# Gated layer: transposed latent scores placed later between the gated pieces than the other latent steps

## The chip, the cores and the metric

The kernel runs on one core of one Trainium2 chip, in one launch. The metric is the device time of one execution in microseconds; each kernel is executed several times and the median counts. A further execution is recorded by the hardware profiler, and all views and rows below come from that one.

## The reference, cut to what matters

The program is a model of four layers on x (4 sequences of 512 tokens with 256 features). Each layer normalises x and adds an attention part and a feed-forward part. Only the third layer (index 2) is touched by the change:

```python
xn = _layernorm(x, axis=-1)
x = x + _L2_attn_ref(xn, ...) + _L2_ffn_ref(xn, ...)
```

`_L2_attn_ref` is a gated recurrent attention with 16 heads. Keys, values, queries, slot scores `s` and gates are products of `xn`; the slot weights are `exp(s)` over a running sum, and the recurrences over time give a softmax over 64 slots and then the values:

```python
p = jnp.exp(s - z)                      # z: cumulative log-sum-exp over time
hk = hk * g_t[:, :, None, :] + k_t[..., None] * p_t[:, :, None, :]
pvT = jax.nn.softmax(okT, axis=-1)
hv = hv * g_t[..., None] + p_t[..., None] * v_t[:, :, None, :]
o = o * rsqrt(mean(o * o) + EPS) * g_norm_weight * (g * sigmoid(g))
return o.reshape(b, t, VALUE_DIM) @ Wo
```

`_L2_ffn_ref` begins with a causal attention over latent keys and queries, again with 16 heads of 16 features, and goes on to a shared expert and seven routed ones:

```python
scores = jnp.einsum('bqhd,bkhd->bhqk', q, k) * scale
scores = jnp.where(causal[None, None], scores, jnp.finfo(scores.dtype).min)
probs = jax.nn.softmax(scores, axis=-1)
out = jnp.einsum('bhqk,bkhd->bqhd', probs, v).reshape(b, s, H)
h = x + out @ o_w
out = h + moe(rmsnorm(h, ln2_w), ...)
```

## The kernel before, in words

All products are in float32 on TensorE (PE); one matmul of the program shows as two instructions in the trace. VectorE (DVE), ScalarE (ACT) and GpSimd (POOL) do the element-wise work. Each engine works through its own queue in order. The order in a queue is made when the program is built: instructions are traced in the order of the Python code, and a scheduler places each on its engine when, by its own costs, its inputs are there.

`layer2` computes the gated attention in 32 units. A unit is one pair of heads and one sequence of 512 tokens. While a unit is computed by `gated_unit`, the next unit's projections are made by `gated_supply` and the previous unit's output product by `gated_drain`. All three are generators that yield after a piece of work. `run` takes their pieces in a fixed pattern (`"mmmmsmsmmdmmsmsdmsd"`, 19 pieces of a unit, where m is the unit, s the supply and d the drain) and places steps of a further generator between them, by a credit that starts at zero in each unit:

```python
credit += rate
while credit >= 1:
    credit -= 1
    next(beside, None)
```

For units 0 to 23 this further generator is `latent_chain`, the latent attention with its shared expert, and the rate is `beside` = 0.44. What is left of the chain after unit 23 is traced at once. For the units after that it is the routed experts, at a rate of their own.

`latent_chain` goes over 16 groups: 4 sequences of 4 groups, each with 4 heads. Three stages overlap. In iteration n, `latent_keys` makes `kT` and `qT` of group n, `latent_maxima` works on group n-1 and `latent_values` on group n-2, the latter two in turns of one step each.

- `latent_maxima` computes the scores with the query in the partitions (`qk`, L2158), in three banks: the last query chunk against 512 keys, the chunks of 384 and 128 keys, the chunk of 256 keys. Four tiles, one for each head, are filled at a time. DVE reads each tile with one or two fused instructions that mask it and keep the row's maximum (`junk`, `mx`, L2165). At the end the negated maxima are transposed (`mxt`, L2175) and added to a spare row of `qT` (L2176), so that later scores come out with the maximum subtracted.
- `latent_values` computes the same scores transposed, with the key in the partitions (`kq`, L2190), in three banks of the same sizes (512; 384 with 128; 256). ACT takes the exponential of each of the four tiles (`pr`, L2195), POOL zeroes what lies above the diagonal (L2198). Then `pv` (L2206) is the product with the values, `pvs` (L2212) its copy, and `pvt` (L2216) the transposition back.

All PSUM tiles of the latent chain come from one pool of four buffers, `pw` (tag `w`). A bank of `qk` takes all four, and so does a bank of `kq`. So `kq` of a bank can start only when DVE has read the tiles of `qk` before it, and the next `qk` only when ACT has read those of `kq`. The gated units have a pool of four PSUM buffers of their own.

The gated work that lies between these steps: `pj` (L1763, projections), `turn` (L1794), `sc` (L1826, scores; DVE masks them at L1832), `pt` (L1841, values and gates by tokens), `st` (L1814, sums), `pok` (L1859, L1865), `okt` (L1874), `pvt` (L1894), `pov` (L1905, L1911), `ot` (L1947) and `o` (L1954, added to x by DVE at L1959). On DVE the slot sums run through a scan (L1775) and four reciprocals (L1776), and the softmax over slots through L1878, L1880 and L1883. ACT changes its function table between the exponentials and the silu of the gates (L1890).

Of the kernel before, what the change touches and what calls it, by code (L numbers as in the profile page):

```python
# [14 lines left out]
P = 128  # L15
NB = 4
T = 512
# [29 lines left out]


BLOCK = {0: 0, 1: 512, 3: 896, 2: 1024}
BANKS = ((0, (0,)), (512, (1, 3)), (1024, (2,)))  # L50


# [78 lines left out]
class Net:  # L131
# [1009 lines left out]
    def layer1(self):  # L1141
# [115 lines left out]
        self.stats = self.small  # L1257
        self.ordered.close()

    def arms1(self, m, counts):  # L1260

        which = self.r1["which"]
        index = self.nc.values_load(
            which[0:1, m : m + 1], min_val=0, max_val=len(counts) - 1,
            skip_runtime_bounds_check_because="a count of as many numbers at most",
        )
        for i in self.tc.Switch(index, len(counts)):
            yield counts[i]
# [308 lines left out]
    def layer2(self):  # L1577

        nc, a = self.nc, self.a
        UNITS = 8 * NB

        first, beside = 24, 0.44
        moe = self.moe2
        with ExitStack() as ctx:
            tp = lambda n, bufs, **k: ctx.enter_context(self.tc.tile_pool(name=n, bufs=bufs, **k))
            self.ahead = tp("gaw", 2), tp("gaw2", 2)
            self.weights = weights = {0: self.gated_weights(0)}
            self.gp = gp = {"wk": tp("ga", 1), "wk2": tp("ga2", 2), "ps": tp("gaps", 4, space=PSUM)}  # L1590
            gp["gn"] = gn = gp["wk"].tile([P, 1], F32, tag="gn", name="gn")
            self.load(gn, a["l2_gn"])
            units = {}

            def supplied(u):
                pair, b = 2 * (u // 8) + u % 2, u % 8 // 2
                for _ in norms[b]:
                    pass
                if pair not in weights:
                    weights[pair] = self.gated_weights(pair)  # L1600
                units[u] = {"b": b, "w": weights[pair]}
                return self.gated_supply(units[u])

            def supplies(u):
                yield from supplied(u)

            def normed(b):
                if b:
                    with self.tc.issue_after(marks[b - 1]):
                        for _ in collects[b]:  # L1610
                            pass
                    self.layer_norm(b)
                marks.append(self.mark)
                yield
                self.to_features(
                    gp["ps"], self.xn[:, 4 * b : 4 * b + 4, :], self.xnT[:, :, b * T : (b + 1) * T], tag="ps"
                )
                yield

            def run(u, beside, rate):  # L1620


                supply = supplies(u + 1) if u + 1 < UNITS else iter(())
                gathered = collects.get(u // 2 + 1, iter(())) if u < 6 else iter(())
                drain = self.gated_drain(units[u - 1]) if u else iter(())
                credit = 0.0
                chains = {"m": self.gated_unit(units[u]), "s": supply, "d": drain}
                for n, what in enumerate("mmmmsmsmmdmmsmsdmsd" if u + 1 < UNITS else "mmmmdmmdmmdmmm"):
                    next(chains[what], None)
                    if n % 8 != 7:  # L1630
                        with self.tc.issue_after(marks[min(u // 2, NB - 1)]):
                            next(gathered, None)
                    credit += rate
                    while credit >= 1:
                        credit -= 1
                        next(beside, None)

            marks = []
            collects = {b: self.collect1(b, 5) for b in range(1, NB)}
            norms = [normed(b) for b in range(NB)]  # L1640
            for it in (norms[0], supplied(0)):
                for _ in it:
                    pass
            with ExitStack() as lctx:
                lp = self.lp
                lp["wk"] = lctx.enter_context(self.tc.tile_pool(name="la", bufs=1))
                lp["w"] = lctx.enter_context(self.tc.tile_pool(name="laps", bufs=4, space=PSUM))
                latent = self.latent_chain()
                for u in range(first):
                    run(u, latent, beside)  # L1650
                for _ in latent:
                    pass
            wk = tp("ex", 4)
            gp["ex"] = tp("exps", 4, space=PSUM)
            self.router3()
            routed = self.routed2(wk)
            for u in range(first, UNITS - 2):
                run(u, routed, 1.45)
            for _ in routed:
                pass  # L1660
            run(UNITS - 2, self.ended2(wk, gp["ex"]), 0.75)
            run(UNITS - 1, self.ahead3(gp["ex"]), 1.0)
            drain = self.gated_drain(units[UNITS - 1])
            for chain in (self.units3[0], self.units3[0], drain, self.units3[0], drain, drain):
                next(chain, None)
        self.held.close()
# [381 lines left out]
    def latent_chain(self):  # L2048


        self.latent_tables()
        ready, maxed = None, None
        for n in range(4 * NB + 2):
            values, maxima = maxed, ready
            maxed, ready = maxima, None
            b, g = n // 4, n % 4
            if b < NB:
                if g == 0:
                    yield from self.latent_inputs(b)
                ready = b, g, *self.latent_keys(g)  # L2060
                yield
            steps = []
            if maxima:
                steps.append(self.latent_maxima(*maxima[2:]))
            if values:
                if values[1] == 0:
                    self.latent_va()
                    yield
                steps.append(self.latent_values(*values))
            while steps:  # L2070
                for s in list(steps):
                    if next(s, None) is None:
                        steps.remove(s)
                    yield
            if values and values[1] == 3:
                yield from self.latent_output(values[0])
                yield from self.experts2(values[0])
# [67 lines left out]
    def latent_maxima(self, kT, qT):  # L2145


        nc, lp = self.nc, self.lp
        wk, pw = lp["wk"], lp["w"]
        mx = self.small.tile([P, 4, 4], F32, tag="lmx", name="mx")  # L2150
        for cs in ((3,), (2, 0), (1,)):
            tiles = [pw.tile([P, T], F32, tag="w", name="qk") for _ in range(4)]
            offs = [sum((i + 1) * P for i in cs[:m]) for m in range(len(cs))]
            for off, c in zip(offs, cs):
                m = (c + 1) * P
                for j in range(4):
                    r = slice(32 * j, 32 * j + 32)
                    nc.tensor.matmul(  # L2158
                        tiles[j][:, off : off + m], qT[r, c * P : (c + 1) * P], kT[r, :m], start=True, stop=True
                    )  # L2160
            for j in range(4):
                for off, c in zip(offs, cs):
                    m = (c + 1) * P
                    junk = wk.tile([P, T], F32, tag="q1", name="junk")
                    nc.vector.tensor_tensor_reduce(  # L2165
                        out=junk[:, :m], in0=tiles[j][:, off : off + m], in1=self.hide[:, T - m :],
                        op0=ALU.add, op1=ALU.max, scale=1.0, scalar=NEG, accum_out=mx[:, c, j : j + 1],
                    )
            yield True

        mt = lp["mt"]
        nc.vector.tensor_scalar(mt.rearrange("q c (j r) -> q c j r", r=32)[:, :, :, 16], mx, -1.0, None, ALU.mult)
# [5 lines left out]
    def latent_values(self, b, g, kT, qT):  # L2178

        nc, lp = self.nc, self.lp  # L2180
# [3 lines left out]
        for off, js in BANKS:  # L2184
            m = sum(T - i * P for i in js)
            tiles = [pw.tile([P, T], F32, tag="w", name="kq") for _ in range(4)]
            for i in js:
                for j in range(4):
                    r = slice(32 * j, 32 * j + 32)
                    nc.tensor.matmul(  # L2190
                        tiles[j][:, BLOCK[i] - off : BLOCK[i] - off + T - i * P], kT[r, i * P : (i + 1) * P],
                        qT[r, i * P :], start=True, stop=True,
                    )
            for j in range(4):
                nc.scalar.activation(pr[:, j, off : off + m], tiles[j][:, :m], AF.Exp, scale=0.25)  # L2195
            for i in js:
# [2 lines left out]
                    out=d, in_=d, compare_op=ALU.is_ge, fill=0.0, base=0, pattern=[[0, 4], [1, P]],  # L2199
                    channel_multiplier=-1,  # L2200
                )
            yield True
        pv = pw.tile([P, T], F32, tag="w", name="pv")
        for i in range(4):
            for j in range(4):
# [4 lines left out]
                )  # L2210
        pvs = wk.tile([P, T], F32, tag="pvs", name="pvs")
        nc.scalar.copy(pvs, pv)  # L2212
        yield True
        pt = pw.tile([P, 4, P], F32, tag="w", name="pvt")
        for c in range(4):
            nc.tensor.transpose(pt[:, c, :], pvs[:, c * P : (c + 1) * P], self.ident)  # L2216
# [407 lines left out]
```

## Time and profile before

| | |
|---|---|
| median of 3 runs | 2164.0 us (2156.78 to 2164.17) |
| the profiled execution's own time | 2162.52 us |
| its span, first to last instruction | 2160.8 us |
| mean granted PE clock | 0.931 |
| busy: PE, DVE, ACT, POOL | 1963.7, 1181.5, 831.8, 612.3 us |
| first and last `kq` matmul (L2190) | 505.9 and 1439.5 us from the span's start |

The page divides the span into 40 slices of 54 us and gives the busy share of each engine in tenths. Its groups of instructions name the line, the engine, the operation, what is written and read, the count, the busy time, the mean of one in ns, and after the last bar the idle time of the engine just before them with what ended it. PEld is the loading of weights into PE, which overlaps with the matmuls. The starts and ends of matmuls are modelled: a matmul that waits after it was issued is drawn long. In a view of one line, "sat idle before it until" lists the releasers, each with microseconds and number of times. In the timeline a row is start, length, engine, line, operation, tiles, count, and in brackets the idle time before it.

### The profile page before, as it was taken

Reading aid. Unit: us, or ns where it says so; the run is one execution under the profiler, and the core shown is the slowest. Engines: PE = TensorE matmul, PEld = TensorE weight load, DVE = VectorE, ACT = ScalarE, POOL = GpSimd, SP = SyncE. Lnnn points to the kernel's source line nnn. Section 1 sums busy time; section 2 is a strip of 40 time slices with the busy share of each in tenths; the row PEclk is TensorE's granted clock in tenths of the full one; section 3 lists DMA queues with packets and bytes.
Section 4 is the critical chain, followed back from the end, with each engine's and each line's share of the span. In section 5 each row is a group of like instructions: output and inputs, shape, how many; then the busy total and the mean of one; then the engine's idle time right before and its main releaser. Section 6 shows DMA issues by size and latency. Waiting matters only on the chain.

```text
span 2160.8 us, 35450 instructions
## 1 busy us (share of the span) xinstructions
PE 1963.7 (91%) x13049; PEld 1450.8 (67%) x13049; DVE 1181.5 (55%) x3462; ACT 831.8 (38%) x1688; POOL 612.3 (28%) x727
## 2 busy tenths in 40 slices
PE   6867996689999999999999999989999978899995
PEld 2556875455666766667666676657877866688894
DVE  4886753586655554655565655636556564413223
ACT  2443353323444433434344433342445434425221
POOL 5325652472111111112112111121444451112231
PEclk9958997779999999999999999987999989899998
DMA  9425965320000000000000000102433220267696
GB/s 295 135 98 171 292 186 180 109 67 13 1 1 18 18 11 1 1 1 13 18 11 6 1 1 17 34 11 81 130 117 119 78 73 1 99 210 259 229 335 229
DMA packets 149644, 198.22 MB, mean 92 GB/s; under 512 B 16981, under 2 KB 127672, under 8 KB 149304
## 3 DMA queue, kind: packets, MB, share of 16 engines
q1 hardware_dynamic: 135320, 156.42, 22.3%
q0 software_dynamic: 14112, 39.15, 5.9%
q8 instruction: 111, 1.82, 0.3%
q14 instruction: 101, 0.83, 0.1%
HBM read 154.23 MB, written 41.29 MB: 90 GB/s over the span
## 4 chain that ended last, share of the span: by engine, by line
PE 56%; DVE 9%; issue 7%; POOL 6%; DMA 3%; ACT 2%; another core or an unknown queue 1%; SPq 0%; POOLq 0%; DVEq 0%; ACTq 0%
PE pt L1841 8%; PE pj L1763 6%; PE g L2375 4%; PE o L1954 4%; PE kq L2190 3%; PE sc L1826 3%; PE pov L1905 2%; DVE junk L2165 2%; PE qk L2158 2%; PE o L2388 2%; PE pv L2206 2%; DMA r<-l_rows,in_slot 1%; PE st L1814 1%; PE turn L1794 1%; PE pok L1859 1%
## 5 line engine op out<-in xcount | busy, mean ns | idle before, releaser
L2165 DVE CUSTOM_DVE_ANT_0 junk<-qk,hide 128x512 f32<-128x512 f32 (+3 forms) x256 | 124.5, 486 | 42.2 <-PE qk L2158 25.1
L2198 POOL TENSOR_SCALAR_AFFINE_SELECT pr<-pr 128x512 f32<-128x512 f32 x64 | 40.2, 640 | 339.6 <-ACT pr L2195 339.6
L2375 PEld LDWEIGHTS g<-rT,we 128*128 128x128 f32 x1120 | 132.0, 194 | 5.5 <-ACT rT L382 3.4
L2375 PE MATMUL g<-rT,we 128*128 128x128 f32 x1120 | 132.7, 277 | 2.2 <-ACT rT L382 2.2
L1841 PE MATMUL pt<-Wg,xnT 128*128 128x256 f32 x512 | 124.4, 395 | 2.4 <-DVE both L367 1.0
L349 POOL DMA_INDIRECT r<-l_rows,in_slot x73 | 71.1, 974 | 190.4 <-PE rt L380 106.7
L389 POOL DMA_INDIRECT l_outs<-y,to x73 | 72.1, 988 | 184.9 <-ACT y L388 151.1
L1954 PE MATMUL o<-Wo,oT 128*128 128x256 f32 x512 | 121.9, 381 | 0.0
L1832 DVE TENSOR_TENSOR s<-sc,keep 128x512 f32<-128x512 f32 x128 | 82.5, 683 | 71.8 <-PE sc L1826 68.8
L1841 PE MATMUL pt<-Wv,xnT 128*128 128x256 f32 x512 | 120.7, 387 | 0.0
L1776 DVE RECIPROCAL rz<-rz 128x128 f32<-128x128 f32 x128 | 116.8, 933 | 0.4
L1841 PEld LDWEIGHTS pt<-Wg,xnT 128*128 128x128 f32 x512 | 97.0, 196 | 27.0 <-issue 7.7
L361 DVE TENSOR_TENSOR mine<-r,number 128x2 f32<-128x2 f32 x73 | 13.2, 181 | 179.5 <-DMA r<-l_rows,in_slot 179.4
L2195 ACT ACTIVATE pr<-kq 128x512 f32<-128x512 f32 (+1 forms) x192 | 86.3, 529 | 51.6 <-PE kq L2190 51.2
L1841 PEld LDWEIGHTS pt<-Wv,xnT 128*128 128x128 f32 x512 | 95.3, 191 | 15.2 <-issue 0.2
L1409 POOL DMA_INDIRECT r<-l_rows,in_slot x84 | 82.6, 984 | 67.4 <-PE rt L1421 38.4
L1954 PEld LDWEIGHTS o<-Wo,oT 128*128 128x128 f32 x512 | 96.1, 197 | 8.3 <-issue 0.5
L2190 PE MATMUL kq<-q,kT 32*128 32x128 f32 (+3 forms) x512 | 91.0, 505 | 7.6 <-DVE mx L2165 6.2
L1844 ACT COPY v<-pt 128x512 f32<-128x512 f32 x64 | 37.3, 586 | 127.5 <-PE pt L1841 126.4
L1922 DVE TENSOR_TENSOR o<-pov,g 128x512 f32<-128x512 f32 x64 | 41.3, 686 | 77.0 <-ACT sq L1921 76.0
L2190 PEld LDWEIGHTS kq<-q,kT 32*128 32x128 f32 x512 | 41.7, 197 | 51.4 <-DVE mx L2165 33.8
L1927 POOL TENSOR_TENSOR rs<-ms,sm 128x8 f32<-128x8 f32 x32 | 6.5, 204 | 240.6 <-DVE ms L1925 240.5
(566 smaller groups left out, 4606.3 us busy)
## 6 DMA issues: line engine op xcount, KB each, us to landing
we<-l_w SPq DMA_DIRECT2D x70, 512.0 KB
we<-l_wo SPq DMA_DIRECT2D x35, 512.0 KB
l_outs<-none SPq DMA_DIRECT2D x1, 11776.0 KB
l_outs<-y SPq DMA_DIRECT2D x42, 256.0 KB
we<-l_r_gate SPq DMA_DIRECT2D x38, 128.0 KB
we<-l_r_up SPq DMA_DIRECT2D x38, 128.0 KB
we<-l_r_down SPq DMA_DIRECT2D x38, 128.0 KB
l_rows<-xn SPq DMA_DIRECT2D x8, 544.0 KB
```

The costliest lines, as they stand in the source:

```text
L349: self.nc.gpsimd.indirect_dma_start(out=r[:, m, :], out_offset=None, in_=moe["rows"][:, :], in_offset=bass.IndirectOffsetOnAxis(ap=moe["in ...
L389: self.no_order(moe["name"] + " back", nc.gpsimd.indirect_dma_start(out=moe["outs"][:, :], out_offset=bass.IndirectOffsetOnAxis(ap=to, axi ...
L1409: nc.gpsimd.indirect_dma_start(out=r[:, i, :], out_offset=None, in_=moe["rows"][:, :], in_offset=bass.IndirectOffsetOnAxis(ap=moe["in_slot ...
L1763: nc.tensor.matmul(ps, w[n][:, k, :], self.xnT[:, k, t["b"] * T : (t["b"] + 1) * T], start=(k == 0), stop=(k == KD - 1))
L1776: inverse = lambda c: nc.vector.reciprocal(rz[:, c * P : (c + 1) * P], rz[:, c * P : (c + 1) * P])
L1832: nc.vector.tensor_tensor(s, ps[hh], keep4, ALU.mult)
L1841: nc.tensor.matmul(ps[:, i, :], self.xnT[:, k, s : s + P], w[n][:, k, :], start=(k == 0), stop=(k == KD - 1))
L1954: nc.tensor.matmul(ps[:, p, :], of_parity(oT[:, h, c * D : (c + 1) * D], p), wo[:, h, :], start=(h == 0), stop=(h == 1),)
L2165: nc.vector.tensor_tensor_reduce(out=junk[:, :m], in0=tiles[j][:, off : off + m], in1=self.hide[:, T - m :], op0=ALU.add, op1=ALU.max, sca ...
L2190: nc.tensor.matmul(tiles[j][:, BLOCK[i] - off : BLOCK[i] - off + T - i * P], kT[r, i * P : (i + 1) * P], qT[r, i * P :], start=True, stop= ...
L2195: nc.scalar.activation(pr[:, j, off : off + m], tiles[j][:, :m], AF.Exp, scale=0.25)
L2375: nc.tensor.matmul(pt[:, m, :], we[:, q, k * T + m * P : k * T + (m + 1) * P], rT[:, k, :], start=(k == 0), stop=(k == KD - 1),)
```

## The change

`latent_chain` and its stages now yield a number with each step. `run` takes it off the credit beside the 1 of the step itself: a positive number puts the next latent step later, a negative one puts it earlier. Each bank of `latent_maxima` yields +0.3 (`SPARE`), so that what follows it, the bank of `kq` in `latent_values`, comes later. The bank of `kq` yields -0.1, and the key step, the end of the maxima, the product `pv` and the end of the values yield -0.15 each. Over one full iteration the numbers add up to zero. Steps without a number count as before. The rate goes from 0.44 to 0.455.

Besides, each `kq` matmul is now traced within `issue_after(behind)`, where `behind` is the last PE instruction that was traced before the bank (found by the new method `latest`). This is an edge of order within PE's queue: the scheduler can no longer place the `kq` matmuls ahead of that instruction. No arithmetic is changed.

```diff
+SPARE = 0.3
...
+    def latest(self, engine):
+        engine = getattr(mybir.EngineType, engine)
+        return next(i for i in reversed(self.nc.cur_bb.bb.instructions) if i.engine == engine)
...
-        first, beside = 24, 0.44
+        first, beside = 24, 0.455
...
                     while credit >= 1:
-                        credit -= 1
-                        next(beside, None)
+                        credit -= 1 + (next(beside, None) or 0.0)
...
                 ready = b, g, *self.latent_keys(g)
-                yield
+                yield -SPARE / 2
...
                 for s in list(steps):
-                    if next(s, None) is None:
+                    spare = next(s, None)
+                    if spare is None:
                         steps.remove(s)
-                    yield
+                    yield -SPARE / 2 if spare is None else spare
...
(latent_maxima, after each bank)
-            yield True
+            yield SPARE
...
(latent_values)
             tiles = [pw.tile([P, T], F32, tag="w", name="kq") for _ in range(4)]
+            behind = self.latest("PE")
             for i in js:
                 for j in range(4):
                     r = slice(32 * j, 32 * j + 32)
-                    nc.tensor.matmul(
+                    with self.tc.issue_after(behind):
+                        nc.tensor.matmul(
...
-            yield True
+            yield -SPARE / 3
         pv = pw.tile([P, T], F32, tag="w", name="pv")
...
         nc.scalar.copy(pvs, pv)
-        yield True
+        yield -SPARE / 2
```

In the text below a round is one iteration of `latent_chain` in which both a `qk` and a `kq` group are worked on; there are fifteen. The cover of a bank is the time of the gated matmuls that stand on PE between its `qk` and its `kq`, or between its `kq` and the next `qk`.

More of the change, by code (lines that the diff above doesn't have):

```diff
@@ L2189, in latent_values @@
                     r = slice(32 * j, 32 * j + 32)
[L2190 to L2193, printed above, removed]
+                    with self.tc.issue_after(behind):
+                        nc.tensor.matmul(
+                            tiles[j][:, BLOCK[i] - off : BLOCK[i] - off + T - i * P], kT[r, i * P : (i + 1) * P],
+                            qT[r, i * P :], start=True, stop=True,
+                        )
             for j in range(4):
```

## The prediction

> **What bounds the kernel now.** I read the page first, then the busy time by stretches, then who waits in the stage that the change touches, then the timeline of one bank.
>
> ```profile
> PE 1963.7 (91%) x13049; PEld 1450.8 (67%) x13049; DVE 1181.5 (55%) x3462; ACT 831.8 (38%) x1688; POOL 612.3 (28%) x727
> PE   6867996689999999999999999989999978899995
> L2165 DVE CUSTOM_DVE_ANT_0 junk<-qk,hide 128x512 f32<-128x512 f32 (+3 forms) x256 | 124.5, 486 | 42.2 <-PE qk L2158 25.1
> ```
>
> ```profile
> 500.00:1440.00 940.00, 927.55 (x6432) 630.43 (x6430) 540.47 (x1278) 377.30 (x705) 158.25 (x185) 0.98 0.03 9
> 836.60:843.40 6.80, 6.80 (x31) 3.38 (x30) 0.43 (x1) 2.66 (x5) 1.22 (x2) 0.58 0.00 0
> 952.70:962.90 10.20, 10.20 (x36) 7.63 (x40) 4.34 (x17) 5.06 (x8) 1.22 (x2) 0.55 0.00 0
> 1058.50:1061.90 3.40, 3.40 (x26) 3.14 (x25) 0.00 (x0) 0.78 (x2) 1.22 (x2) 0.67 0.00 0
> ```
>
> The columns of the second fence are length, then busy time of PE, PEld, DVE, ACT and POOL, granted clock, DMA. From 500 to 1440 us the gated units carry the latent chain, and PE is the bound: 927.6 of 940 us. That 99% hides waits, because a matmul that waits for a free PSUM buffer is drawn long. What each scores line waited for, first L2190 (kq), then L2158 (qk), over the run:
>
> ```profile
>   DVE mx L2165: 40.0, 63
> ```
>
> ```profile
>   ACT pr L2195: 4.7, 15
> ```
>
> One bank in the timeline, PE, then DVE, then ACT:
>
> ```profile
> 553.70 1.14 PE L2158 MATMUL qk<-kT,q 32*128 32x512 f32 x8
> 554.77 0.66 PE L1794 MATMUL turn<-ident,kT 128*128 128x128 f32 x4
> 555.26 1.90 PE L1954 MATMUL o<-Wo,oT 128*128 128x256 f32 x8
> 557.09 2.31 PE L2190 MATMUL kq<-q,kT 32*128 32x512 f32 x8
> ```
>
> ```profile
> 555.01 0.68 DVE L2165 CUSTOM_DVE_ANT_0 junk<-qk,hide 128x512 f32<-128x512 f32 x1
> ...
> 558.15 0.08 DVE L2165 DVE_READ_ACCUMULATOR2_ANT mx<- 128x1 f32 x1
> ```
>
> ```profile
> 558.29 1.28 ACT L2195 ACT_TABLE_LOAD   x1 [2.19 <-PE kq L2190]
> 559.59 2.06 ACT L2195 ACTIVATE pr<-kq 128x512 f32<-128x512 f32 x4
> ```
>
> The latent pool has four buffers. qk fills all four, DVE empties them (554.8 to 558.2, 3.4 us), and only 2.3 us of gated matmuls stand before kq. So kq takes 2.3 us instead of the 1.1 us that the same matmuls take where nothing is late. The rule of this stage: **stall = DVE time after qk minus the PE work between qk and kq**. Applied to the fifteen rounds with their three banks it gives 15.1 us for the 512 banks, where the timeline shows 15.7. In all, kq is 44.6 us long-winded in this stage: 15.7 (512), 24.2 (384 with 128), 4.7 (256). That is the most that later scores can win directly.
>
> **The change, part by part.** The order edge on kq holds matmuls behind an earlier matmul of the same queue, so it adds no wait of its own. Rate 0.44 to 0.455: a unit has 19 pieces and credit starts at zero in each, so 8.4 or 8.6 steps become 8 either way. In both built programs the chain's remainder stands behind unit 23. No cost. No DMA moves on SP; POOL swaps one row of selects. Two copies of `a2T` go from DVE to ACT, of about 0.4 us each, under PE's work.
>
> The spares move the kq steps about one piece later and the others earlier. The order in which each program issues on PE, with the gated groups at their durations in the timeline (turn 0.5, half of o 1.7, pt 3.5, pj 1.8, sc 1.1, first pov 1.9), gives the cover between qk and kq, in us, rounds 1 to 15 of the 512 bank. Before: 4.0 2.2 2.1 2.9 4.5 3.6 5.0 2.4 4.0 2.2 2.1 2.9 4.5 3.6 2.1. After: 4.4 3.4 2.1 5.8 6.3 3.6 5.0 4.2 5.0 3.4 2.1 5.8 6.3 3.6 2.9. The timeline starts kq about 0.15 later than these sums.
>
> The DVE side: bare time is 3.4 us for the 512 bank (four maxima 0.85 us apart, as in the timeline above), 4.0 for the 384, 2.2 for the 256. DVE's queue mixes gated work into it. That work, counted between first and last maximum of a bank, is 12.6, 15.7 and 7.7 us over all rounds before, and 14.1, 16.4 and 9.3 after. So the need hardly falls, and the gain is the cover alone.
>
> - 512 banks: rounds 2, 4, 8, 10 and 12 lose their stall. Round 1 keeps 3.2 - 2 x 0.93 (two reciprocals of 934 ns, L1776, fall behind the last maximum) + 0.5 (pvt, no longer ahead) = 1.9. Rounds 3 and 11 are issued as before, 2.0 each. Rounds 9 and 15 keep 0.5 and 0.4. Sum 6.8, gain 8.9.
> - 384 banks: what stays is 1.9, 1.2, 0.5, 4.1, 3.9, 1.2, 0.5, 3.1, 1.3 in rounds 1, 3, 5, 6, 8, 11, 13, 14, 15. Rounds 6 and 14 keep theirs because the maxima queue on DVE behind scan, reciprocals and softmax of the gated unit, and kq stays at the same place against that work. Sum 17.7, gain 6.5.
> - 256 banks: round 7 gets worse, since its first kq has 1.5 us of cover instead of 2.1 and 4.1 us of gated DVE work among its maxima instead of 2.2: about 3.0 for 1.3. Rounds 5 and 13 keep 0.3. Sum 3.6, gain 1.1.
>
> Gain on kq: 16.5 us. Against it stands the other half of the same interval: kq to the next qk, where qk waits for ACT's four exponentials (2.1 us, or 3.5 from kq's end with a table load of 1.28). Cover after for qk 384: 2.3 4.5 4.0 1.6 2.4 1.1 6.3 2.4 2.9 4.5 4.0 1.6 2.4 1.1 4.4. With needs of 2.4 or 3.5 as each round shows now, rounds 4, 5, 6, 8, 9, 12, 13, 14 stall by 1.75, 0.95, 1.15, 0.5, 0.45, 1.75, 0.95, 1.15: 8.7 us, 3.8 now, so 4.9 lost. qk 256 loses 0.45 in three rounds, 1.4. In round 8 ACT is ordered exp, table load, silu, table load, exp: two loads more, 2.6 us on ACT, of which the 2.2 us of PE cover leave about 1. Cost 7.3.
>
> Of the other queues that a kq step is moved past, POOL's selects (0.64 us each) are what pv (L2206) needs: between the last kq and pv stand 3.4 us in rounds 4 and 12, 6.2 before, and the exponentials and the select take about 2.2. Hidden; without that cover it would be 2 us a round. The key steps move earlier, with their products on DVE and the sum on POOL (1.27 us); they are read a round later, so nothing waits.
>
> The three half-clock spells in the second fence each begin at or just behind a kq stall. The one at 1058.5 follows the round 9 stalls (1.5 and 2.3 us), which go; 3.4 us at half speed is 1.7 us won. Rounds 6 and 8 keep their stalls and spells.
>
> [...]
>
> [...]
>
> Sum: 16.5 - 7.3 + 1.7 = 10.9 us. The profiled execution took 2162.5 us (span 2160.8 and 1.7 around it), 1.5 under the median of 2164.0. So 2151.6 for it, and 2153 for a median. No row shows the gated chain's own waits in the new order: they are some 13 us in the stage now (among them 1.8 before the round 8 kq), and I take them as unchanged, with 5 either way.
>
> **The rivals.**
> *Slower: the wait goes over to ACT.* PE's queue is in order, so time given to DVE before kq is taken from ACT before qk. If every bank needs the table load (3.5 us), the covers above leave 12.4 us of stall on qk 384, and those of qk 256 (1.5 to 6.3 us) 14.3: 26.7 against 3.8 now. That is 22.9 lost for 16.5 won, and the two stalls over 2 us may halve the clock, 3.4 more: about 10 slower, 2174. It decides once ACT costs over 18 us. Against it: 18 loads on L2195 now serve 48 banks, and the new order has one more there.
> *No change.* DVE stays as late as the gated work ahead of it, and moved scores only wait elsewhere. Then only rounds with a bare DVE side win: 4.3 (512), 2.5 (384), less 7.3: 2164. For it: rounds 3, 6, 11 and 14, where the change does not do what it says at all.
> *More.* DVE time falls to the bare values. Stalls left are 2.7, 4.9 and 0.6: gain 36, less 7.3, and the spells of rounds 6 and 8 (17 us at half speed, 8.5) go: about 39 won, 2125.
>
> **How the numbers follow.** Forecast (8 to 20 us won) 0.5; no change 0.27; slower 0.13; more 0.1. About 0.5%, 10.8 us, is what a measurement of this kernel can tell from no change, and the forecast lies on that edge. So faster by more takes 0.37 of the forecast's 0.5 and all of the 0.1, 0.47; within it 0.37; slower by more 0.16 with the tail of no change. The range leaves out the far ends of "more" and "slower": 2133 to 2170.
>
> **What would show it.** Right: L2190's wait on L2165 falls from 40 to about 25 us, L2158's wait on L2195 rises from 4.7 to about 10, the round 2 kq 512 takes 1.1 us, rounds 6 and 8 still show a half clock, and the spell of round 9 is gone. Wrong: the wait on L2165 stays near 40, or L2158 waits over 18 us on ACT, or gated lines (L1763, L1814, L2206) show new waits of over 5 us.

## The result, and the profile after

The changed kernel takes 2170.7 us (median of 11 executions, 2167.3 to 2177.7), the kernel before 2164.0 us beside it (11 executions). The ratio is 1.0036, 95% interval 1.0023 to 1.0049: some 7 us slower, where 2153 was forecast. The profiled execution of the changed kernel took 2177.69 us (span 2175.9), the slowest of its eleven, so differences between the two profiled executions come out larger than those between the medians.

First the lines of the page that answer to those shown of before: busy time of the engines and the two groups of the latent scores that were slow, the maxima and kq. The lines of the program have moved: qk is L2163, its maxima L2170, kq L2197, its exponentials L2202; the gated sums st are L1818, the masks of the gated scores L1836.

```profile
PE 1968.9 (90%) x13049; PEld 1459.9 (67%) x13049; DVE 1180.8 (54%) x3460; ACT 834.1 (38%) x1692; POOL 612.4 (28%) x727
L2170 DVE CUSTOM_DVE_ANT_0 junk<-qk,hide 128x512 f32<-128x512 f32 (+3 forms) x256 | 124.3, 485 | 47.5 <-PE qk L2163 31.1
L2197 PE MATMUL kq<-q,kT 32*128 32x128 f32 (+3 forms) x512 | 71.1, 486 | 5.3 <-DVE mx L2170 4.5
```

kq fell from 91.0 us busy and 7.6 idle to 71.1 and 5.3. What each scores line sat idle for over the run, first kq, then qk:

```profile
  DVE mx L2170: 20.5, 27
```

```profile
  ACT pr L2202: 11.8, 37
```

The wait of kq on DVE was 40.0 us in 63 pieces and is 20.5 in 27; the wait of qk on ACT was 4.7 and is 11.8. Both were forecast (about 25 and about 10). The bank shown in the prediction, round 2, in the timeline of PE:

```profile
549.40 1.14 PE L2163 MATMUL qk<-kT,q 32*128 32x512 f32 x8
550.47 1.98 PE L1767 MATMUL pj<-xnT,Wq 128*128 128x512 f32 x4
552.38 1.16 PE L1830 MATMUL sc<-q,eF 64*128 64x128 f32 x16
553.47 0.66 PE L1798 MATMUL turn<-ident,kT 128*128 128x128 f32 x4
554.06 1.14 PE L2197 MATMUL kq<-q,kT 32*128 32x512 f32 x8
```

Now 3.5 us of gated work stand between the end of qk and kq instead of 2.3, and kq takes 1.14 us instead of 2.31. The change does here exactly what it says. So the time was lost elsewhere. The view of who waits, PE in the stretch from 480 to 1440 us (what waited, for what, us, times, longest):

```profile
PE st L1818 <- DVE s L1836: 7.6, 2, 3.8
```

No such line is in the answer for before. The timeline of that place, PE, then DVE:

```profile
722.08 3.72 PE L1845 MATMUL pt<-Wv,xnT 128*128 128x256 f32 x16
729.62 0.57 PE L1818 MATMUL st<-eT,kt 128*64 128x64 f32 x12 [3.82 <-DVE s L1836]
730.22 2.84 PE L1767 MATMUL pj<-xnT,Wk 128*128 128x512 f32 x4
```

```profile
721.09 0.69 DVE L1963 TENSOR_TENSOR x<-o,x 128x512 f32<-128x512 f32 x1 [0.24 <-PE o L1958]
728.09 0.88 DVE L2093 SCALAR_TENSOR_TENSOR xn<-xn,rms,ln 128x256 f32<-128x256 f32 x2 [6.30 <-POOL rms L436]
728.88 1.28 DVE L1836 TENSOR_TENSOR s<-sc,keep 128x512 f32<-128x512 f32 x2
730.08 0.87 DVE L2093 SCALAR_TENSOR_TENSOR xn<-xn,rms,ln 128x256 f32<-128x256 f32 x2
```

Read it from DVE. At 721.8 DVE is free, and the scores that the masks (L1836) read are there at 722.1. But two of the four scalings of an RMS norm (L2093, the first step of the expert block at the end of a sequence) stand ahead of the masks, and they wait 6.30 us for a factor that POOL computes. DVE works through its queue in order and does nothing in these 6.30 us. The masks free the PSUM buffers of the gated scores, so PE's st waits too, 3.82 us. The same happens at 1271 us, and both times PE runs at half clock afterwards: the projection pj at 730.22 takes 2.84 us, where it took 1.98 in the bank above. Windows of the whole core, with the granted clock in the third column from the end:

```profile
731.40:734.80 3.40, 3.40 (x12) 1.93 (x13) 0.81 (x2) 0.58 (x1) 0.00 (x0) 0.53 0.00 0
836.00:850.00 14.00, 12.71 (x84) 8.91 (x83) 9.70 (x31) 8.79 (x13) 1.22 (x2) 1.00 0.00 1
1054.00:1076.00 22.00, 22.00 (x178) 15.62 (x176) 14.04 (x40) 10.74 (x21) 5.71 (x7) 1.00 0.08 26
1270.80:1277.60 6.80, 6.63 (x30) 4.02 (x32) 2.71 (x8) 1.01 (x3) 0.00 (x0) 0.52 0.00 0
```

The spells of rounds 6 and 9 (836.6 and 1058.5 before) are gone, and new ones stand behind the two waits of st.

Three numbers from each trace serve for the comparisons below. *Stage* is the time from the fourth to the twenty-fifth group of `pj<-xnT,Ws`, 21 units with the latent chain beside them. *Half clock* is what that stage lost to the granted clock: the length of each record below full clock times what is missing of it. *kq* and *qk* are the busy times of the two scores lines over the run, in which their waits are contained.

| kernel | ratio to before (95%) | stage | half clock | kq | qk | kq+qk |
|---|---|---|---|---|---|---|
| before | 1 | 858.6 | 13.7 | 91.0 | 59.8 | 150.8 |
| after | 1.0036 (1.0023 to 1.0049) | 877.6 | 23.9 | 71.1 | 69.0 | 140.1 |
| after, again | 1.0031 (1.0015 to 1.0047) | 872.4 | 18.8 | 71.6 | 69.5 | 141.1 |
| rate alone | 1.0122 (1.0101 to 1.0144) | 892.0 | 27.3 | 89.3 | 62.9 | 152.2 |
| edge alone | 1.0016 (0.9997 to 1.0035) | 860.0 | 15.4 | 90.2 | 59.5 | 149.7 |
| spares alone (rate 0.44, no edge) | 0.9983 (0.9970 to 0.9996) | 858.4 | 18.8 | 72.6 | 80.1 | 152.7 |
| after, rate 0.44 | 0.9971 (0.9958 to 0.9984) | 856.8 | 17.1 | 73.1 | 79.9 | 153.0 |
| after, masks first | 1.0008 (0.9993 to 1.0023) | 862.6 | 13.7 | 72.3 | 69.2 | 141.5 |
| rate alone, masks first | 1.0070 (1.0045 to 1.0095) | 876.4 | 15.4 | 88.1 | 62.3 | 150.4 |
| after, rate 0.45 | 0.9948 (0.9930 to 0.9965) | 857.3 | 15.4 | 70.6 | 65.9 | 136.5 |
| SPARE 0.35 | 0.9923 (0.9905 to 0.9940) | 847.5 | 8.5 | 65.5 | 72.3 | 137.8 |
| SPARE 0.35, rate 0.45 | 0.9933 (0.9914 to 0.9951) | 855.7 | 15.4 | 66.2 | 68.4 | 134.6 |
| SPARE 0.4 | 0.9887 (0.9870 to 0.9904) | 849.2 | 8.5 | 60.9 | 77.7 | 138.6 |
| SPARE 0.45 | 0.9983 (0.9956 to 1.0010) | 858.3 | 11.9 | 61.9 | 76.3 | 138.2 |

### The profile page after: what moved, and what is told of

Same layout as the page of the kernel before. It is cut to its first block, busy times and chain, and to the rows that moved or that the text cites. A ratio compares the mean times of both kernels' runs of the same rounds, so it can differ in the third digit from the quotient of the medians.

```text
span 2175.9 us, 35439 instructions
## 1 busy us (share of the span) xinstructions
PE 1968.9 (90%) x13049; PEld 1459.9 (67%) x13049; DVE 1180.8 (54%) x3460; ACT 834.1 (38%) x1692; POOL 612.4 (28%) x727
## 4 chain that ended last, share of the span: by engine, by line
PE 58%; DVE 10%; issue 6%; POOL 4%; DMA 3%; ACT 3%; SPq 0%; another core or an unknown queue 0%; DVEq 0%; POOLq 0%; ACTq 0%
PE pt L1845 8%; PE pj L1767 7%; PE o L1958 4%; PE g L2382 4%; PE sc L1830 3%; PE pov L1909 2%; PE kq L2197 2%; DVE junk L2170 2%; PE qk L2163 2%; PE o L2395 2%; PE pv L2213 2%; PE st L1818 1%; DMA r<-l_rows,in_slot 1%; DVE rz L1780 1%; PE turn L1798 1%
## 5 line engine op out<-in xcount | busy, mean ns | idle before, releaser
L2170 DVE CUSTOM_DVE_ANT_0 junk<-qk,hide 128x512 f32<-128x512 f32 (+3 forms) x256 | 124.3, 485 | 47.5 <-PE qk L2163 31.1
L1845 PE MATMUL pt<-Wg,xnT 128*128 128x256 f32 x512 | 130.3, 408 | 6.5 <-DVE pv L1884 2.5
L350 POOL DMA_INDIRECT r<-l_rows,in_slot x73 | 71.1, 974 | 192.7 <-PE rt L381 108.7
L1836 DVE TENSOR_TENSOR s<-sc,keep 128x512 f32<-128x512 f32 x128 | 82.3, 682 | 60.3 <-PE sc L1830 57.3
L2202 ACT ACTIVATE pr<-kq 128x512 f32<-128x512 f32 (+1 forms) x192 | 86.3, 530 | 29.4 <-PE kq L2197 28.7
L2197 PE MATMUL kq<-q,kT 32*128 32x128 f32 (+3 forms) x512 | 71.1, 486 | 5.3 <-DVE mx L2170 4.5
L2163 PE MATMUL qk<-kT,q 32*128 32x256 f32 (+3 forms) x512 | 69.0, 482 | 6.6 <-DVE mx L2170 3.9
L1925 ACT ACTIVATE sq<-pov 128x512 f32<-128x512 f32 x64 | 34.7, 595 | 103.0 <-PE pov L1915 90.5
```

The costliest lines, as they stand in the source:

```text
L1836: nc.vector.tensor_tensor(s, ps[hh], keep4, ALU.mult)
L1845: nc.tensor.matmul(ps[:, i, :], self.xnT[:, k, s : s + P], w[n][:, k, :], start=(k == 0), stop=(k == KD - 1))
L2163: nc.tensor.matmul(tiles[j][:, off : off + m], qT[r, c * P : (c + 1) * P], kT[r, :m], start=True, stop=True)
L2170: nc.vector.tensor_tensor_reduce(out=junk[:, :m], in0=tiles[j][:, off : off + m], in1=self.hide[:, T - m :], op0=ALU.add, op1=ALU.max, sca ...
L2197: nc.tensor.matmul(tiles[j][:, BLOCK[i] - off : BLOCK[i] - off + T - i * P], kT[r, i * P : (i + 1) * P], qT[r, i * P :], start=True, stop= ...
```

## The experiments

Theory A: the spares win on kq about what was forecast, and the new rate loses it again, because it moves single steps to places where DVE's queue has something late at its head. Theory B: the moved scores themselves lose behind kq what they win before it, and the rate is nothing.

**The parts, each alone.** The rate alone, in the kernel before:

```diff
-        first, beside = 24, 0.44
+        first, beside = 24, 0.455
```

> The kernel before with the rate 0.455 in place of 0.44 and nothing else. Theory A (the rate is what costs): the credit now reaches 4, 5 and 8 one piece earlier in each unit, so two RMS scalings of the expert block stand ahead of the score masks on DVE in two of the four sequences. They wait some 6 us for POOL's rms as in the kernel after, the masks come late, PE's st stands 4 us at each of the two places and runs at half clock behind it: 8 to 18 us slower than before, 2172 to 2182. The wait of kq on DVE stays near 40 us. Theory B (the moved scores cost: what is won before kq is lost behind it): the rate alone does nothing, 2164, within 4 us, and the st line waits no more than in the kernel before.

Measured: 1.0122, 26 us slower, more than the whole change and more than theory A's range. The waits of PE show the same line as the kernel after, here L1832 and L1814:

```profile
PE st L1814 <- DVE s L1832: 7.7, 2, 3.8
```

and DVE's queue the same order:

```profile
720.71 0.88 DVE L2088 SCALAR_TENSOR_TENSOR xn<-xn,rms,ln 128x256 f32<-128x256 f32 x2 [6.30 <-POOL rms L435]
721.51 1.28 DVE L1832 TENSOR_TENSOR s<-sc,keep 128x512 f32<-128x512 f32 x2
```

Why a rate that leaves eight steps in a unit does this: the credit passes 4, 5 and 8 at pieces 10, 12 and 19 with 0.44, and at pieces 9, 11 and 18 with 0.455. Three of the eight steps come one piece earlier in every unit. Where such a step is the first of the expert block, its scalings are placed on DVE before the masks of the next scores.

The kernel after with the old rate:

```diff
-        first, beside = 24, 0.455
+        first, beside = 24, 0.44
```

> The kernel after with the rate set back to 0.44; the spares and the order edge stay. Theory A: the masks stand ahead of the scalings again, the 4 us stalls of st go, and what the later scores win is left: 2150 to 2158. Theory B: the rate is nothing, so the time stays that of the kernel after, 2168 to 2173, and the waits behind kq are as in the kernel after.

Measured: 0.9971, 6 us faster than before and 14 faster than the kernel after. Theory B is out as to the rate. Yet theory A wanted 2150 to 2158 against 2164, a ratio of 0.993 to 0.997, and this is its weak end. The table shows why: kq falls by 17.9 us, but qk grows by 20.1. At the old rate theory B is right about the spares: what is given to DVE before kq is taken from ACT before qk. The wait of qk on ACT, 4.7 us before, is now

```profile
  ACT pr L2202: 13.0, 43
```

So the 6 us are not explained by the two scores lines, which together take 2.2 us more than before. The stage is 1.8 us shorter than in the kernel before and the two units behind it 3.9 us longer (145.5 against 141.6). Where the gain arises, these traces do not show.

The order edge alone, and the spares without it (both as edits of the kernel after):

```diff
-SPARE = 0.3
+SPARE = 0.0
...
-        first, beside = 24, 0.455
+        first, beside = 24, 0.44
```

> The kernel before with the order edge on kq alone (all spares zero, rate 0.44). Both theories: no change, 2164 within 4 us, since the scheduler rarely places kq ahead of what was traced before it. If the edge is what costs (a third theory), 2168 or more.

```diff
-                    with self.tc.issue_after(behind):
+                    if True:
...
-        first, beside = 24, 0.455
+        first, beside = 24, 0.44
```

> The spares alone, without the order edge and at rate 0.44. Theory A: as the kernel after at rate 0.44, 2150 to 2158, and kq's wait on DVE falls from 40 us to some 25. Theory B: kq's wait falls as far, but the time is 2168 to 2173, with the loss in qk's wait on ACT and in the gated lines.

Measured: 1.0016 and 0.9983. The edge does nothing. The order on every engine is that of before in the first of these, and that of the after kernel at rate 0.44 in the second, but for single instructions behind unit 23 that change places. The two are therefore repetitions (1 and 1.0016, 0.9971 and 0.9983), and show that about 0.15% is what two equal programs can differ by here.

**The head of DVE's queue.** In the kernel after, the scalings are traced one piece later and held behind the masks by an edge of order on DVE. On PE, ACT, POOL and SP nothing moves, and on DVE only the two pairs of masks that stood behind the scalings.

```diff
-        for i in range(4):
-            nc.vector.scalar_tensor_tensor(dst[:, i, :], src[:, i, :], rs[:, i : i + 1], weight, ALU.mult, ALU.mult)
+        def scale():
+            self.held_scale = None
+            with self.tc.issue_after(self.masked) if dst is src else ExitStack():
+                for i in range(4):
+                    nc.vector.scalar_tensor_tensor(
+                        dst[:, i, :], src[:, i, :], rs[:, i : i + 1], weight, ALU.mult, ALU.mult
+                    )
+        if dst is src:
+            self.held_scale = scale
+        else:
+            scale()
...
                     next(chains[what], None)
+                    if self.held_scale:
+                        self.held_scale()
...
                 nc.vector.tensor_tensor(s, ps[hh], keep4, ALU.mult)
                 out.append(s)
+            self.masked = self.latest("DVE")
             return out
```

> The kernel after, with the RMS scalings of the expert block held behind the gated score masks on DVE; on every engine the order is that of the kernel after but for the two places where the two masks now stand ahead of the two scalings. Theory A (the head of DVE's queue is the cost): the two waits of st on the masks (7.6 us together) go, and with them the half clock behind them (four spells of 6.8 us and 3.4 us at half speed between 731 and 748 and between 1271 and 1291 us, some 10 us lost), so 10 to 17 us faster than the kernel after: 0.991 to 0.999 of the kernel before, near 0.996. Theory B (the stalls belong to the denser order, whatever stands first on DVE): the stall moves to the transposition of the scaled rows (tr) or the next gated line, and the time stays at 1.002 to 1.005 of before.

Measured: 1.0008, against 1.0036 and 1.0031 for the kernel after. In the trace DVE masks first and waits for POOL afterwards:

```profile
720.78 1.29 DVE L1839 TENSOR_TENSOR s<-sc,keep 128x512 f32<-128x512 f32 x2 [0.39 <-PE sc L1833]
726.71 1.67 DVE L2101 SCALAR_TENSOR_TENSOR xn<-xn,rms,ln 128x256 f32<-128x256 f32 x4 [4.64 <-POOL rms L436]
```

```profile
724.33 0.57 PE L1821 MATMUL st<-eT,kt 128*64 128x64 f32 x12
```

st no longer waits, and the transposition of the scaled rows, which theory B wanted to stall in its place, waits 0.43 us there. The stage is 10 to 15 us shorter than in the two profiles of the kernel after. By the ratios it is 0.25% or 5 us, with intervals that reach from about 1 to 10; that is not far above the 0.15% by which equal programs differed. The next run repeats the edit in another kernel, with a larger effect. So the order of masks and scalings on DVE is a cause, shown with nothing else moved in the stage, but it is not the whole of the rate's cost.

The same edit in the run with the rate alone (there the method `latest` is added too):

```diff
-        first, beside = 24, 0.44
+        first, beside = 24, 0.455
...
+            with self.tc.issue_after(self.masked) if dst is src else ExitStack():
```

> The kernel before at rate 0.455, with the RMS scalings held behind the score masks; otherwise its order on every engine is that of the run with the rate alone (1.0122 of before). Theory A: st's 7.7 us of waits go and most of the half clock behind them, 10 to 17 us: 1.004 to 1.008 of before. That would leave 8 to 16 us of the rate's cost in other places (gated lines whose DVE inputs are late). Theory A in its strong form (the two scalings are the whole cost of the rate): 0.998 to 1.002. Theory B: no change, 1.010 to 1.014.

Measured: 1.0070 against 1.0122: 11 us won, in theory A's first range. The strong form, that the two scalings are all, falls: 15 us remain. In that trace PE waits for DVE in other gated lines that the kernel before hardly waits at, such as

```profile
PE sc L1833 <- DVE q L1906: 4.2, 3, 1.8
PE pt L1849 <- DVE pv L1888: 3.3, 4, 1.2
```

But much the same waits stand in the trace of a fast kernel (rate 0.45 with the spares, the next run: 1.8 us for sc and 3.2 us for pt), so they are not shown to be the rest of the cost. Where the 15 us arise stays open.

**Other doses.** Rate 0.45 in the kernel after. Without the spares the credit would pass 4 and 8 early but 5 not:

```diff
-        first, beside = 24, 0.455
+        first, beside = 24, 0.45
```

> The kernel after with rate 0.45 in place of 0.455, a dose between 0.44 and 0.455. The credit still reaches 4 and 8 a piece earlier than at 0.44, but no longer 5; in the built program the masks stand ahead of the scalings. Worked out by the prediction's rule from the order on PE, the stalls of kq come to 22.7 us and those of qk to 10.6, against 23.8 and 18.3 with the spares at 0.44 (0.9971 of before). Theory A: no st stall, 4 to 9 us faster than at 0.44: 0.993 to 0.996 of before, the fastest so far. Theory B (any rate above 0.44 costs because the chain is denser): 1.000 or more.

Measured: 0.9948, inside the range that the prediction's rule gave. Against rate 0.44 qk falls from 79.9 to 65.9 us, so a higher rate is what the spares need on their other side. It also keeps the chain from falling behind: in the two units that follow the stage, 96 matmuls of pv are left at 0.44 with the spares and 64 at 0.45, and those units take 145.5 and 136.6 us (the kernel before has 64 too, and 141.6 us). So a higher rate suits the spares, but at `SPARE` 0.3 its last 0.005 costs 0.9%. The scalings ahead of the masks, which come with it, are 0.25% of that. The rest was not isolated; the table has kq and qk together 5.0 us lower at rate 0.45 than in the kernel after with the masks first.

Larger spares: in the first run `SPARE` alone, in the second with rate 0.45, in the third 0.4 in place of 0.35 at rate 0.455.

```diff
-SPARE = 0.3
+SPARE = 0.35
```

> The kernel after with SPARE 0.35 in place of 0.3; the rate stays 0.455. In the built program the masks stand ahead of the RMS scalings in all four sequences, by chance of the credits. Theory A (what costs is where single steps fall, the scalings ahead of the masks above all, not the rate as such): no wait of st on the masks, and by the prediction's rule from PE's order 13.0 us of stall before kq and 16.0 before qk, 29.0 together, against 33.3 at SPARE 0.3 and rate 0.45 (0.9948 of before): 0.991 to 0.996. Theory B (a rate of 0.455 costs whatever stands first on DVE): 1.000 to 1.004.

> SPARE 0.35 and rate 0.45. Masks ahead of the scalings. By the rule 16.5 us before kq and 12.4 before qk, 28.9 together: theory A 0.991 to 0.996, some 4 us under SPARE 0.3 at the same rate. Theory B: between that run and the kernel after, 0.995 to 1.003.

> SPARE 0.4 at rate 0.455: scores later still. Masks ahead of the scalings. By the rule kq's stalls fall to 10.7 us and qk's rise to 20.6, 31.3 together. If what is given to DVE is taken from ACT, as the sum says, this is no better than SPARE 0.35: 0.993 to 0.998, with kq's stalls smaller and qk's larger in its trace. If later is simply better, it is the fastest, under 0.992.

Measured: 0.9923, 0.9933 and 0.9887. The first two times are as theory A expected: at `SPARE` 0.35 rate 0.455 is no slower than 0.45. So 0.455 as such is not what costs. But the order is not the one that was expected. With 0.35 and 0.4 at rate 0.455 the scalings do stand ahead of the masks in two of the four sequences, the same two as in the kernel after, only further ahead of them. With 0.4, DVE, then PE:

```profile
699.90 1.67 DVE L2093 SCALAR_TENSOR_TENSOR xn<-xn,rms,ln 128x256 f32<-128x256 f32 x4 [1.69 <-POOL rms L436]
...
704.48 1.27 DVE L1836 TENSOR_TENSOR s<-sc,keep 128x512 f32<-128x512 f32 x2
```

```profile
703.25 1.16 PE L1830 MATMUL sc<-qT,kT 64*128 64x128 f32 x16
```

The scalings wait 1.69 us for POOL instead of 6.30, three other steps of DVE follow them, and only then are the scores there (704.4); the masks run at once. By these traces what matters is not which of the two stands first, but whether the one at the head is late while the other is ready.

The third run is a miss. The traces do show the exchange that was foretold, kq's wait on DVE down to 12.0 us and qk's wait on ACT up to 21.9 (11.8 in the kernel after), first kq, then qk:

```profile
  DVE mx L2170: 12.0, 17
```

```profile
  ACT pr L2202: 21.9, 61
```

but kq and qk together are at 138.6 us, no less than in the runs beside it (137.8 and 134.6). What the two faster kernels at rate 0.455 have in common is the half clock: 8.5 us lost against 13.7 before and 15.4 at rate 0.45. Why 0.4 is faster than 0.35 by 8 us the traces do not say: its stage is no shorter, and 6.4 of the 8.1 us between the two profiles lie ahead of the stage (it begins at 514.7 and at 521.1 us). SPARE 0.4 is the fastest version found, 1.1% under the kernel before.

The kernel after once more, beside these on the same chip:

> The kernel after once more, beside the runs with other spares on the same chip: 1.002 to 1.005 of before, with the same waits of st on the masks (7.6 us in two places), since the order of the instructions is fixed; what may differ is how many spells of half clock follow them.

Measured: 1.0031, and the st wait is again 7.6 us in two places; 18.8 us are lost to half clock instead of 23.9. The wait repeats, the spells behind it vary.

Last a dose that is later still, and has all four scalings directly ahead of the masks in two sequences:

```diff
-SPARE = 0.3
+SPARE = 0.45
```

> SPARE 0.45 at rate 0.455: scores later again than with 0.4 (0.9887 of before). But by where the credits fall, two sequences have all four RMS scalings ahead of the score masks on DVE, as the kernel after has two of them; with 0.4 none has. Worked out from PE's order, 10.0 us of stall before kq and 22.5 before qk, 32.5 together, against 31.3 with 0.4. Theory A (the head of DVE's queue): st waits for the masks again, 3 to 5 us at two places, with half clock behind it, so 6 to 18 us are lost against SPARE 0.4: 0.991 to 0.997. Theory C (how late the scores are is all that counts): 0.985 to 0.990 and no wait of st.

Measured: 0.9983. Later scores alone (theory C) are out: kq and qk are as with 0.4 (138.2 us), and 20 us are gone, a little more than theory A allowed. But not by the wait that I had expected. DVE waits at the head of its queue as before; on PE the transposition tr now stands directly behind pt and takes the wait, ahead of st:

```profile
715.10 1.67 DVE L2093 SCALAR_TENSOR_TENSOR xn<-xn,rms,ln 128x256 f32<-128x256 f32 x4 [6.25 <-POOL rms L436]
716.69 1.28 DVE L1836 TENSOR_TENSOR s<-sc,keep 128x512 f32<-128x512 f32 x2
```

```profile
715.64 1.73 PE L479 MATMUL tr<-ident,xn 128*128 128x128 f32 x8 [2.78 <-DVE xn L2093]
717.43 0.57 PE L1818 MATMUL st<-eT,kt 128*64 128x64 f32 x12
718.03 3.68 PE L1767 MATMUL pj<-xnT,Wk 128*128 128x512 f32 x4
```

Over the stage tr waits 8.1 us, against 3.2 with 0.4. But from 0.4 to 0.45 the order changes in dozens of places on PE and on DVE, not only here, and the stage is 9 of the 20 us longer. So this run supports the reading but does not isolate it as the two runs with the masks first do.

## Why the prediction was wrong, step by step

- *The rule for kq, gain 16.5 us: right, and a little low.* Counted from the first to the last matmul of a bank, as the prediction's 44.6 us are, the 512 banks keep stalls of 2.0, 1.9, 1.0, 1.9 and 0.2 us in rounds 1, 3, 9, 11 and 15, 7.1 in all, where 6.8 was forecast, and rounds 2, 4, 8, 10 and 12 take their bare 1.14. The 384 banks keep 15.1 instead of 17.7 (round 6 keeps 1.4, not 4.1, and round 8 6.2, not 3.9), the 256 banks 3.0 instead of 3.6: some 19 us won.
- *The ACT side, cost 7.3 us: right.* qk 384 stalls in rounds 4, 5, 6, 8, 12, 13 and 14 by 1.1 to 1.4 us, 8.4 in all (8.7 forecast), 4.6 more than before. qk 256 loses 3.2 instead of 1.4, and qk 512, which was given nothing, 1.1. Together 9 us.
- *"Rate 0.44 to 0.455 ... 8.4 or 8.6 steps become 8 either way ... No cost": this is the step that failed.* The count is right; where the steps fall on the engines other than PE was not looked at. Rate 0.44 in the changed kernel is worth 14 us, and in the kernel before the rate alone costs 26. Of this, 5 and 11 us are shown to be the scalings that wait for POOL at the head of DVE's queue; where the rest arises stays open. The step was wrong on the gaining side too: with the spares, rate 0.45 leaves 32 matmuls of pv fewer to the units behind the stage than 0.44 does (9 us there) and gives room before qk.
- *The gated chain's own waits, "unchanged, with 5 either way": failed with it.* The sum followed the queue of PE bank by bank and that of DVE only between the maxima. The expert block, whose scalings went ahead of the masks, was in none of the terms, although its order on DVE is fixed when the program is built. The prediction named this as what would make it wrong (L1814 with a new wait of over 5 us: 7.6).
- *The clock, 1.7 us won: wrong in sign.* The spell of round 9 went as said, and that of round 6 too, which was said to stay. But there are new spells, those behind the two waits of st among them, and the stage lost 23.9 us to half clock (18.8 in the second profile) instead of 13.7.
- *The order edge, no cost: right* (the order is the same without it).

The rivals named ACT as the place of a loss. The slower one decides at a cost of 18 us on qk; 9 came, and the part of the loss that is shown lay in DVE's queue. But its mechanism is real: at rate 0.44 qk takes back all that kq wins. So the 6 us won there are not the forecast's sum come true.

On the clock: in the traces of before and after each spell below full clock in the stage is at 0.50 and lasts 3.4, 6.8 or 10.2 us. What starts one, and how long a wait has to be for it, was not shown. In the run with SPARE 0.45 a spell begins at 718.1, 2.5 us behind the end of the wait of 2.78 us shown above, and in that run the longest wait of PE from 480 to 1440 us is 2.8. The projection pj at 718.03 takes 3.68 us, against 1.98 at full clock.

## What to carry to other kernels

A rate that places steps of one generator between those of another is not a count: work out at which piece each step falls before and after, and follow every step that moves through the queue of each engine, not only the one that bounds. Look for an instruction with a late input at the head of an in-order queue: in the kernel after, DVE stood idle for 6.30 us at the scalings while the masks behind them were ready. Where the result of such an instruction is not urgent, an edge of order that puts the ready work first can pay: here it gave back 5 and 11 us, and the work put behind waited 0.43 us on PE. When a wait is traded between two engines, add up both sides: in the changed kernel kq and qk together moved by half of what kq alone did (10.7 of 19.9 us), and at rate 0.44 they rose by 2.2.

## What the runs showed of the hardware

I had not expected how unevenly waits and half clock go together. Many short ones went with less half clock than a few long ones: with SPARE 0.4, qk waits 21.9 us for ACT in 61 pieces (0.36 us each), and 8.5 us are lost to half clock; in the kernel after two waits of 3.8 us have four spells behind them, 23.9 us together and 11.9 lost (the kernel before has one of 3.4 us at the first of these places). No experiment isolated this. The same program also loses different amounts from one execution to the next (23.9 and 18.8 us for the kernel after), so a single profiled execution can stand several microseconds off the median (2177.7 against 2170.7).
